# Routing logits of a mixture-of-experts stage: gate weights as the stationary operand, four column quadrants, and a transpose back

## The chip, the core and the metric

The kernel runs on one core of a Trainium2 chip. The metric is device time in microseconds of one execution; lower is better. A core has five engines with instruction queues of their own, each worked off in order: TensorE (PE; matmuls, with PEld for its weight loads), VectorE (DVE), ScalarE (ACT), GpSimd (POOL) and SyncE (SP, which here only issues DMAs). A matmul takes a stationary operand (the weights, loaded into the array first) and a moving operand (streamed through it column by column), and writes to PSUM.

## What is computed

All of it is f32, on 2 x 2048 tokens of 256 features, four residual steps in a row:

```python
x = x + attn_a(layernorm(x))      # causal attention, 16 heads of 16
x = x + ffn(layernorm(x))         # mixture of experts, first pass
x = x + attn_b(layernorm(x))      # softplus mixer, token by token
x = x + ffn(layernorm(x))         # the same mixture of experts, second pass
```

The mixture of experts, with E = 8 experts and the best two per token:

```python
logits = xt @ gate_w.T + gate_b                 # [tokens, 8]
scores = softmax(logits)
top_w, top_i = top_k(scores, 2)
gate_dense = sum(one_hot(top_i, 8) * top_w[..., None], axis=1)
outs = [(silu(xt @ w1[e].T + b1[e]) * (xt @ w3[e].T + b3[e])) @ w2[e].T + b2[e] for e in experts]
y = einsum('etd,te->td', outs, gate_dense)
z = silu(xt @ ws1.T + bs1) * (xt @ ws3.T + bs3) @ ws2.T + bs2      # shared expert, 512 wide
out = y + z
```

The change concerns the first line, the logits.

## The kernel before

**Stages.** The tokens are cut into eight chunks of 512 (`CH`), four per batch `b`; a chunk is four blocks of 128 tokens (`NB = 4`). X stays in SBUF throughout. Attention is the first stage. The second stage holds both passes of the mixture of experts (`f` is 0 or 1; the text calls them layer 0 and layer 1) and the mixer between them.

**Work of the second stage.** Generators emit its instructions:

- `route(f, c)` for one chunk: layer norm, transposes of the normalized tokens into feature-major form (`flipped`, tile `flip`, line 706, copied by ScalarE to `xT` at line 709), the gate's matmuls (line 736, tile `psl`), the add of the bias to the logits `lg` (line 741), and the ranks of the eight logits against each other (`ge`, lines 748 and 752) from which each token's two best experts come.
- `sort` and `weigh` for one batch: places in a list ordered by expert, and the softmax weights.
- `scatter` and `combine`: GpSimd's indirect DMAs that put the tokens in that order into DRAM (`xs`, line 868) and fetch the experts' results back (`yg`, line 895), which VectorE adds (line 908).
- `shared(f, c)`: the shared expert of one chunk (tiles `s`, line 986, and `sy`, line 1003).
- `routed(f, b)`: the experts, 39 blocks of 128 sorted tokens (loads at line 1035, transposes `tr` at 1045, copies `turned` at 1050, first matmuls `eu` at 1060, second matmuls `ed` at 1084).
- `mixer(c)`: the softplus step (matmuls `psz` at 936; the three ScalarE passes at 948, 949 and 959).

**Order.** The schedule is written out by the program itself, and each engine runs what it is given in that order. `shared` and `routed` are main work: one step of each in turn. `routing`, `moving` (scatter and combine) and `mixing` are side work. Each `yield (dve, act, pe, pool)` states what the next step is expected to cost on the four engines in us. A planner (`beside`) keeps a planned clock per engine, and after each main step it lets those side steps in whose engines are planned to be free soon and whose predecessor is planned to be done. For a step with a cost on PE the predecessor must be done within 0.2 us of PE's planned clock (`AHEAD`); for VectorE and ScalarE within 1.5 us. So the numbers in a yield decide where the instructions land in the queues, but waits at run time are made by semaphores alone. The routes of a batch run one after the other in one generator; those of layer 1 also wait for the mixer of their chunk, and experts of a batch start when its scatter is placed.

**The gate before.** The chunk's tokens are the stationary operand: for each of four token blocks and each of two halves of the features, 128 x 128 of `xT` are loaded as weights and the 8 columns of `gw_s` move through them. The result has tokens on partitions, 4 x 8 columns of one PSUM bank from `side_bank`, a pool of two banks that flips, gates, sorts and mixers share.

**The loads at the start of the stage.** SyncE issues the loads of `gw`, `gb`, `ws1`, `ws3`, the shared biases, `ws2` and the experts' weights in this order; GpSimd fills constant tiles at the same time.

Of the kernel before, what the change touches and what calls it, by code (L numbers as in the profile page):

```python
# [8 lines left out]
F32 = mybir.dt.float32  # L9
# [7 lines left out]
P = 128  # L17
# [7 lines left out]
NB = CH // P  # L25
NCH = N // CH
TC = B * NCH
E = 8
# [21 lines left out]
def hybrid_block(  # L50
# [23 lines left out]
    nc = tc.nc  # L74

    const = ctx.enter_context(tc.tile_pool(name="const", bufs=1))
    small = ctx.enter_context(tc.tile_pool(name="small", bufs=3))
# [13 lines left out]
    ident = const.tile([P, P], F32, tag="ident", name="ident")  # L91
# [45 lines left out]
    with tc.tile_pool(name="aw", bufs=1) as aw, ExitStack() as aw_ctx:  # L137
# [62 lines left out]
        def spectral(w, u, sp, cols, nm, bank):  # L200

            n = cols // P
            v = aw.tile([P, 2], F32, tag=f"v_{nm}", name=f"v_{nm}")
            for c in range(2):
                nc.vector.tensor_tensor_reduce(
                    wide(f"t_{nm}_{c}")[:, 0:cols], w[:, c, :], u, 1.0, 0.0, ALU.mult, ALU.add, v[:, c:c + 1]
                )
            ps = bank(f"psr_{nm}")
            for m in range(n):
                for c in range(2):  # L210
                    nc.tensor.matmul(
                        ps[:, m:m + 1], w[:, c, m * P:(m + 1) * P], v[:, c:c + 1],
                        start=c == 0, stop=c == 1,
                    )
            r = aw.tile([P, n], F32, tag=f"r_{nm}", name=f"r_{nm}")
            nc.vector.tensor_copy(r, ps[:, 0:n])

            s = aw.tile([P, 2], F32, tag=f"s_{nm}", name=f"s_{nm}")
            nc.vector.tensor_mul(v, v, v)
            nc.vector.tensor_mul(r, r, r)  # L220
            nc.vector.reduce_sum(s[:, 0:1], v, axis=AX.X)
            nc.vector.reduce_sum(s[:, 1:2], r, axis=AX.X)
            ps = bank(f"pss_{nm}")
            nc.tensor.matmul(ps[:, 0:2], ones, s, start=True, stop=True)

            f = aw.tile([P, 1], F32, tag=f"f_{nm}", name=f"f_{nm}")
            ru = aw.tile([P, 1], F32, tag=f"ru_{nm}", name=f"ru_{nm}")
            nc.vector.reciprocal(f, ps[:, 0:1])
            nc.vector.tensor_mul(f, f, ps[:, 1:2])
            nc.gpsimd.tensor_tensor(ru, f, nhalf[:, 0:1], ALU.pow)  # L230
            nc.vector.tensor_mul(f, f, ru)
            nc.vector.reciprocal(f, f)
            nc.vector.tensor_mul(f, f, sp)
            return f

        with ExitStack() as ac:
# [266 lines left out]
            nm, na = 0, 0  # L503
# [7 lines left out]
            f = factors["k"] = spectral(*loaded, 3 * D, "qkv", bank)  # L511
# [9 lines left out]
            while na < len(units) or due or behind:  # L521
# [12 lines left out]
                if run_m:  # L534
# [13 lines left out]
                    kc, i = mx.pick(cols)  # L548
# [19 lines left out]
                if run_m:  # L568
# [10 lines left out]
                    if not mx.left:  # L579
                        shift(*w, mx.part, nmax[nm % 2])  # L580
                        ready[nm] = tick[0] + LAG
                        mx, nm = None, nm + 1
# [3 lines left out]
    fw = ctx.enter_context(tc.tile_pool(name="fw", bufs=1))  # L586
# [8 lines left out]
    def weight(src, shape, nm, eng):  # L595
        t = fw.tile(shape, F32, tag=nm, name=nm)
        eng.dma_start(t, src)
        return t

    def row(src, n, nm, eng):  # L600
        t = fw.tile([P, n], F32, tag=nm, name=nm)
        eng.dma_start(t, src.partition_broadcast(P))
        return t

    gw_s = weight(gw, [P, 2, E], "gw", nc.sync)
    gb_s = row(gb, E, "gb", nc.sync)
    ws1_s = weight(ws1, [P, 2, SH], "ws1", nc.sync)
    ws3_s = weight(ws3, [P, 2, SH], "ws3", nc.sync)
# [48 lines left out]
    def side_bank(nm):  # L657
        return ps_x.tile([P, CH], F32, tag="px", name=nm)
# [8 lines left out]
    def feature_major(nm):  # L667
        while live[0] >= XTS:
            yield None
        live[0] += 1  # L670
        return cw.tile([P, 2, CH], F32, tag="xT", name=f"xT_{nm}", bufs=XTS)

    def token_major(nm):
        while held[0] >= XNS:
            yield None
        held[0] += 1
        return cw.tile([P, NB, D], F32, tag="xn", name=f"xn_{nm}", bufs=XNS)

    def normed(xc, xn, nm):
        st = small.tile([P, NB, 6], F32, tag="lnst", name=f"lnst_{nm}")  # L680
        mv = small.tile([P, NB, 2], F32, tag="lnmv", name=f"lnmv_{nm}")
        ve = small.tile([P, NB], F32, tag="lnve", name=f"lnve_{nm}")
        rs = small.tile([P, NB], F32, tag="lnrs", name=f"lnrs_{nm}")
        for h in range(2):
            yield (0.9, 0, 0, 0)
            for i in range(2 * h, 2 * h + 2):
                nc.vector.bn_stats(st[:, i, :], xc[:, i, :])
                nc.vector.bn_aggr(mv[:, i, :], st[:, i, :])
            if h == 1:
                nc.vector.tensor_scalar_add(ve, mv[:, :, 1], EPS)  # L690
        yield (0, 0, 0, 1.2)
        nc.gpsimd.tensor_tensor(rs, ve, nhalf, ALU.pow)
        for h in range(2):
            yield (0.75, 0, 0, 0)
            for i in range(2 * h, 2 * h + 2):
                nc.vector.tensor_scalar(
                    xn[:, i, :], xc[:, i, :], mv[:, i, 0:1], rs[:, i:i + 1],
                    ALU.subtract, ALU.mult,
                )

    def flipped(xn, xT, nm):
        yield (0, 1.2, 0.9, 0)
        for d in range(2):
            ps = side_bank(f"flip_{nm}_{d}")
            for i in range(NB):
                nc.tensor.transpose(
                    ps[:, i * P:(i + 1) * P], xn[:, i, d * P:(d + 1) * P], ident
                )
            nc.scalar.copy(xT[:, d, :], ps)

    def route(f, c):

        b, q = divmod(c, NCH)
        nm = f"{f}_{c}"
        while f == 1 and c not in mixed:
            yield None
        if q == 0:
            scores[f, b] = rw.tile([P, BLK, E], F32, tag="lg", name=f"lg_{f}_{b}", bufs=1)
            picks[f, b] = rw.tile([P, TOPK, BLK, E], F32, tag="pick", name=f"pick_{f}_{b}", bufs=1)
            sel[f, b] = rw.tile([P, E, BLK], BF16, tag="sel", name=f"sel_{f}_{b}", bufs=1)  # L720
        blk = slice(q * NB, (q + 1) * NB)
        xn = yield from token_major(f"f{nm}")
        yield from normed(X[c], xn, f"f{nm}")
        xhat[f, c] = xn
        yield (0, 0, 0, 2.4)
        nc.gpsimd.tensor_tensor(
            X[c], X[c], bs2_s.unsqueeze(1).to_broadcast([P, NB, D]), ALU.add
        )
        xT = yield from feature_major(f"f{nm}")
        yield from flipped(xn, xT, f"f{nm}")  # L730
        xhatT[f, c] = xT
        yield (0.2, 0, 1.8, 0)
        ps = side_bank(f"psl_{nm}")
        for i in range(NB):
            for d in range(2):
                nc.tensor.matmul(  # L736
                    ps[:, i * E:(i + 1) * E], xT[:, d, i * P:(i + 1) * P], gw_s[:, d, :],
                    start=d == 0, stop=d == 1,
                )
        lg = scores[f, b][:, blk, :]  # L740
        nc.vector.tensor_tensor(
            lg, ps[:, :NB * E].rearrange("p (n e) -> p n e", e=E),
            gb_s.unsqueeze(1).to_broadcast([P, NB, E]), ALU.add,
        )
        yield (1.6, 0, 0, 0)

        ge = small.tile([P, NB, E, E], F32, tag="ge", name=f"ge_{nm}", bufs=2)
        nc.vector.tensor_tensor(
            ge, lg.unsqueeze(2).to_broadcast([P, NB, E, E]),
            lg.unsqueeze(3).to_broadcast([P, NB, E, E]), ALU.is_ge,  # L750
        )
        nc.vector.tensor_tensor(
            ge, ge, before.unsqueeze(1).to_broadcast([P, NB, E, E]), ALU.mult
        )
        up = small.tile([P, NB, E], F32, tag="rup", name=f"rup_{nm}", bufs=2)
        dn = small.tile([P, NB, E], F32, tag="rdn", name=f"rdn_{nm}", bufs=2)
        nc.vector.reduce_sum(up, ge, axis=AX.X)
        nc.vector.reduce_sum(dn, ge.rearrange("p n e j -> p n j e"), axis=AX.X)
        yield (0.6, 0, 0, 0)
        nc.vector.tensor_tensor(up, up, dn, ALU.subtract)  # L760
        pk = picks[f, b]
        for k in range(TOPK):
            nc.vector.tensor_tensor(
                pk[:, k, blk, :], up, level[:, k, :].unsqueeze(1).to_broadcast([P, NB, E]),
                ALU.is_equal,
            )
        nc.vector.tensor_tensor(
            sel[f, b][:, :, blk].rearrange("p e n -> p n e"), pk[:, 0, blk, :], pk[:, 1, blk, :],
            ALU.add,
        )  # L770
# [353 lines left out]
    def routing():  # L1124
        for f, b in rows:
            for c in chunks(b):
                yield from route(f, c)
            yield from sort(f, b)
            yield from weigh(f, b)
# [59 lines left out]
    while sides or todo or shares or mains:  # L1189
# [15 lines left out]
        name = sorted(mains)[turn_of % len(mains)]  # L1205
# [79 lines left out]
```

## Time and profile before

| | us |
|---|---|
| median of 3 runs | 2157.02 (2152.82 to 2159.84) |
| the profiled execution: time | 2150.73 |
| its span, first to last instruction | 2148.8 |
| attention, to the last matmul of its projection | about 1181 |
| second stage, first PE instruction | 1187.1 |
| the 16 gates, first to last | 1191.7 to 1912.8 |
| scatter of the last batch | 1923.5 to 1963 |
| experts of the last batch end on PE | about 2095 |
| last instructions | 2149 |

A page of the profile has busy times of each engine, the span in 40 slices with the busy share of each in tenths, the chain of waits that ended last, and groups of like instructions by source line. A group's line reads: source line, engine, operation, output tile <- input tiles, shapes, count | busy us, mean ns of one | idle time of the engine just before them, and what ended it. Starts and lengths in a timeline or in the chain are us from the span's start. An f32 matmul leaves two records (and two weight loads) on PE, an f32 transpose one. Ends of matmuls are modelled, since they are pipelined, so distances between starts tell more than lengths. TensorE's granted clock was 0.98 of full over the span and 0.98 to 1.00 in the stretches of the second stage between 1187 and 2100 us, except 0.91 from 1960 to 1980.

The gate's own rows, from the groups by line:

| line | engine, operation | count | median ns |
|---|---|---|---|
| 736 | PEld LDWEIGHTS psl, 128x128 | 256 | 192 |
| 736 | PE MATMUL psl, 128x8 moving | 256 | 256 |
| 741 | DVE TENSOR_TENSOR lg, 128x32 | 16 | 191 |
| 748 | DVE TENSOR_TENSOR ge, 128x256 | 16 | 425 |

### The profile page before, as it was taken

The numbers are of one execution on the slowest core, as the hardware profiler recorded it, in microseconds if no ns is written. First come the engines' busy times: TensorE is split into PE (matmuls) and PEld (weight loads), VectorE is DVE, ScalarE is ACT, GpSimd is POOL, SyncE is SP. The second block draws the span as 40 slices with busy tenths as digits, with TensorE's granted clock in tenths as the row PEclk, the third lists the DMA queues.
The fourth block names the chain that finished last, engine by engine and source line by source line (L and its number), as shares of the span: only waits on it lengthen the run. The fifth ranks groups of instructions, "written<-read, shape, count | busy, mean of one in ns | idle before, by whom it ended". The sixth has DMA issues, their size and how long they took to land.

```text
span 2148.8 us, 36170 instructions
## 1 busy us (share of the span) xinstructions
PE 2026.7 (94%) x11840; PEld 1091.1 (51%) x11840; DVE 1384.1 (64%) x3424; ACT 1074.9 (50%) x1566; POOL 872.9 (41%) x1157
## 2 busy tenths in 40 slices
PE   6899999999999999999999999999999999999993
PEld 3444444444444444444444566665656566655662
DVE  2567777777676777777871455545777368763643
ACT  0437577757776757767876122233353234341330
POOL 3325344524444434434445263603432753336305
PEclk9899999999999999999999999999999999999997
DMA  2111110000000000000000511323210332103524
GB/s 93 48 49 36 45 51 16 7 6 6 3 7 6 6 4 4 6 4 4 2 2 1 217 61 64 136 76 118 84 40 25 114 112 85 35 30 131 173 73 122
DMA packets 87587, 113.04 MB, mean 53 GB/s; under 512 B 16368, under 2 KB 75120, under 8 KB 87280
## 3 DMA queue, kind: packets, MB, share of 16 engines
q1 hardware_dynamic: 74000, 75.60, 11.1%
q0 software_dynamic: 12288, 33.57, 4.7%
q8 instruction: 101, 1.65, 0.3%
q10 hardware_dynamic: 1120, 1.57, 0.2%
q14 instruction: 78, 0.64, 0.1%
HBM read 54.59 MB, written 51.64 MB: 49 GB/s over the span
## 4 chain that ended last, share of the span: by engine, by line
PE 80%; DVE 7%; POOL 4%; issue 4%; ACT 3%; DMA 1%; DVEq 0%; SPq 0%; POOLq 0%; ACTq 0%
PE st L378 15%; PE o L397 13%; PE psm L333 13%; PE eu L1060 10%; PE s L986 7%; PE ed L1084 5%; PE sy L1003 4%; PE psk L267 3%; PE tr L1045 2%; PE psz L936 1%; PE psj L446 1%; POOL xs L868 1%; PE psv L293 1%; DVE junk L342 1%; PE psl L736 1%
## 5 line engine op out<-in xcount | busy, mean ns | idle before, releaser
L382 ACT ACTIVATE pt<-st 128x1024 f32<-128x1024 f32 (+3 forms) x640 | 555.8, 895 | 189.8 <-PE psm L333 129.9
L333 PE MATMUL psm<-kT,qT 32*128 32x512 f32 (+3 forms) x2560 | 627.1, 570 | 15.0 <-DMA kT<-sk 8.9
L378 PE MATMUL st<-qT,kT 32*128 32x512 f32 (+3 forms) x2560 | 610.7, 557 | 1.3 <-ACT pt L382 1.3
L347 DVE TENSOR_REDUCE part<-psm 128x1 f32<-128x512 f32 x768 | 477.4, 682 | 121.5 <-PE psm L333 117.3
L408 POOL TENSOR_TENSOR oa<-oa,op 128x512 f32<-128x512 f32 (+3 forms) x288 | 312.8, 1086 | 454.4 <-ACT op L406 454.4
L378 PEld LDWEIGHTS st<-qT,kT 32*128 32x128 f32 x2560 | 266.1, 186 | 225.9 <-ACT pt L382 137.8
L342 DVE CUSTOM_DVE_ANT_0 junk<-psm,maskq 128x384 bf16<-128x384 f32 (+3 forms) x512 | 250.8, 490 | 112.0 <-PE psm L333 47.7
L333 PEld LDWEIGHTS psm<-kT,qT 32*128 32x128 f32 x2560 | 276.1, 186 | 86.2 <-issue 27.1
L397 PE MATMUL o<-pt,v 128*32 128x512 f32 (+3 forms) x2560 | 304.2, 545 | 12.1 <-DVE part L347 5.6
L1060 PE MATMUL eu<-we,turned 128*128 x560 | 263.7, 593 | 0.0
L1067 ACT ACTIVATE es<-ea 128x256 f32<-128x256 f32 x156 | 65.0, 417 | 357.9 <-DVE ea L1065 357.8
L986 PE MATMUL s<-xT_f,ws 128*128 128x512 f32 x512 | 231.4, 595 | 0.0
L895 POOL DMA_INDIRECT yg<-ys,slot x128 | 128.1, 1001 | 234.3 <-DVE x L908 74.0
L385 POOL TENSOR_SCALAR_AFFINE_SELECT pt<-pt 128x256 f32<-128x256 f32 x256 | 102.3, 407 | 211.6 <-ACT pt L382 207.7
L406 ACT COPY op<-o 128x512 f32<-128x512 f32 (+3 forms) x288 | 148.3, 515 | 64.1 <-PE o L397 48.8
L1065 DVE TENSOR_TENSOR ea<-eu,be 128x512 f32<-128x512 f32 x156 | 107.4, 688 | 111.0 <-PE eu L1060 110.4
L1084 PE MATMUL ed<-we,turned 128*128 x624 | 162.6, 383 | 14.5 <-ACT turned L1050 14.5
L397 PEld LDWEIGHTS o<-pt,v 128*32 128x32 f32 x2560 | 52.5, 108 | 218.0 <-DVE part L347 123.4
L1084 PEld LDWEIGHTS ed<-we,turned 128*128 128x128 f32 x624 | 116.2, 190 | 87.9 <-issue 48.3
L868 POOL DMA_INDIRECT xs<-xn_f,slot x128 | 124.7, 974 | 85.1 <-DVE slot L822 57.9
L986 PEld LDWEIGHTS s<-xT_f,ws 128*128 128x128 f32 x512 | 94.8, 191 | 102.0 <-issue 95.4
L1060 PEld LDWEIGHTS eu<-we,turned 128*128 128x128 f32 x560 | 97.6, 191 | 75.0 <-issue 73.1
(266 smaller groups left out, 2111.0 us busy)
## 6 DMA issues: line engine op xcount, KB each, us to landing
xs<-xs SPq DMA_DIRECT2D x156, 128.0 KB
ys<-ey SPq DMA_DIRECT2D x156, 128.0 KB
xs<-zeros SPq DMA_DIRECT2D x78, 128.0 KB
we<-in_we_dram SPq DMA_DIRECT2D x8, 768.0 KB
x<-in_x_dram SPq DMA_DIRECT2D x8, 512.0 KB
kT<-sk SPq DMA_DIRECT2D x128, 32.0 KB
out_dram<-x SPq DMA_DIRECT2D x8, 512.0 KB
be<-in_be_dram SPq DMA_DIRECT2D x1, 3072.0 KB
```

The source lines that it names most:

```text
L333: nc.tensor.matmul(ps[:, :n], self.q[r, i * P:(i + 1) * P], kT[b, g, kc][r, :n], start=True, stop=True,)
L342: nc.vector.tensor_tensor_reduce(junk[:, :n], ps[:, :n], maskq[:, CH - n:], 1.0, LOW, ALU.add, ALU.max, m,)
L347: nc.vector.reduce_max(m, ps[:, :n], axis=AX.X)
L378: nc.tensor.matmul(st[:, i, off:], k[r, ks], q[r, off:], start=True, stop=True)
L382: nc.scalar.activation(pt[:, :, off:], st[:, :, off:], AF.Exp)
L397: nc.tensor.matmul(o[32 * j:32 * j + 32, off:], V[kb // NB][:, kb % NB, 4 * g + j, :], pts[j // 2][:, j % 2, off:], start=True, stop=True,)
L406: nc.scalar.copy(t[:, off:], o[:, off:])
L408: nc.gpsimd.tensor_tensor(a[:, off:], a[:, off:], t[:, off:], ALU.add)
L868: ins = nc.gpsimd.indirect_dma_start(out=XS[b], out_offset=bass.IndirectOffsetOnAxis(ap=slots[f, b][:, k, n:n + 1], axis=0), in_=xhat[f, b ...
L986: nc.tensor.matmul(ps, w[:, d, cs], xT[:, d, :], start=d == 0, stop=d == 1)
L1060: nc.tensor.matmul(ps, t[:, 1, d * P:(d + 1) * P], we_s[:, bass.ds(v + d * CH, CH)], start=d == 0, stop=d == 1,)
L1084: nc.tensor.matmul(ps[:, 0:D], t[:, 0, d * P:(d + 1) * P], we_s[:, bass.ds(v + 2 * CH + d * D, D)], start=d == 0, stop=d == 1,)
```

## The change

- `gw_s` becomes 32 columns wide; GpSimd sets it to zero and the load fills columns 0 to 7 of each half of the features.
- The gate's operands change places. `gw_s` (128 features x 32 columns) is the stationary operand, and 128 tokens of `xT` move. Token block i writes partitions 32 i to 32 i + 31 of the bank (a column quadrant of the array), and the loop over the halves of the features is now outside that over the blocks.
- ScalarE copies the 128 x 128 result to a new SBUF tile `lt` (one buffer), TensorE transposes it into a second side bank, and VectorE adds the bias from there, reading 8 of every 32 columns.
- The planner's step (0.2, 0, 1.8, 0) becomes two: (0, 0.3, 0.6, 0) ahead of the matmuls and the copy, and (0.2, 0, 0.2, 0) ahead of the transpose and the add.
- `ge` has one buffer where it had two.

```diff
-    gw_s = weight(gw, [P, 2, E], "gw", nc.sync)
+
+    gw_s = fw.tile([P, 2, 32], F32, tag="gw", name="gw")
+    nc.gpsimd.memset(gw_s, 0.0)
+    nc.sync.dma_start(gw_s[:, :, 0:E], gw)
...
-        yield (0.2, 0, 1.8, 0)
+        yield (0, 0.3, 0.6, 0)
+
         ps = side_bank(f"psl_{nm}")
-        for i in range(NB):
-            for d in range(2):
+        for d in range(2):
+            for i in range(NB):
                 nc.tensor.matmul(
-                    ps[:, i * E:(i + 1) * E], xT[:, d, i * P:(i + 1) * P], gw_s[:, d, :],
+                    ps[32 * i:32 * i + 32, 0:P], gw_s[:, d, :], xT[:, d, i * P:(i + 1) * P],
                     start=d == 0, stop=d == 1,
                 )
+        lt = small.tile([P, P], F32, tag="lt", name=f"lt_{nm}", bufs=1)
+        nc.scalar.copy(lt, ps[:, 0:P])
+        yield (0.2, 0, 0.2, 0)
+        ps = side_bank(f"pst_{nm}")
+        nc.tensor.transpose(ps[:, 0:P], lt, ident)
         lg = scores[f, b][:, blk, :]
         nc.vector.tensor_tensor(
-            lg, ps[:, :NB * E].rearrange("p (n e) -> p n e", e=E),
+            lg, ps[:, 0:P].rearrange("p (n e) -> p n e", e=32)[:, :, 0:E],
             gb_s.unsqueeze(1).to_broadcast([P, NB, E]), ALU.add,
         )
         yield (1.6, 0, 0, 0)
 
-        ge = small.tile([P, NB, E, E], F32, tag="ge", name=f"ge_{nm}", bufs=2)
+        ge = small.tile([P, NB, E, E], F32, tag="ge", name=f"ge_{nm}", bufs=1)
```

## The prediction of the time

> **What bounds the kernel now.** I read the page's busy shares, its 40 slices and its chain of waits first.
>
> ```profile
> PE 2026.7 (94%) x11840; PEld 1091.1 (51%) x11840; DVE 1384.1 (64%) x3424; ACT 1074.9 (50%) x1566; POOL 872.9 (41%) x1157
> ...
> PE   6899999999999999999999999999999999999993
> ...
> PE 80%; DVE 7%; POOL 4%; issue 4%; ACT 3%; DMA 1%; DVEq 0%; SPq 0%; POOLq 0%; ACTq 0%
> ```
>
> TensorE is busy in every slice but the ends and carries 80% of the chain. The change lies in the second stage, from 1187 us on; attention before it keeps its instructions. So I went to the stage: the chain around one gate (the eight logits matmuls of a 512-token chunk, tile psl).
>
> ```profile
> 1206.58 1.73 PE sy L1003 x8
> 1208.31 1.69 PE psl L736 x16
> 1209.99 2.04 PE sy L1003 x9
> ```
>
> The columns are start, length, engine, tile, line, records (an f32 matmul leaves two records, a transpose one). The gate sits between other matmuls with no hole on either side: what it gives up, the next matmul takes. Summing the holes of over 0.25 us between PE records from 1187 to 2110 us gives 35.6 us, 6.5 of them before the stage's first transposes; nearly everything else is queued PE work. The windows agree: 1187 to 1316 us holds 128.9 us of PE in 129, 1500 to 1700 holds 194.6 in 200, 1700 to 1900 holds 187.8. Sixteen gates at 1.70 us are 27.2 us of PE.
>
> **Why a gate costs 1.70 us.** Each of its 16 records streams 8 columns only, but loads 128 columns of tokens as weights. The records start 0.112 us apart, the pace of the loads (LDWEIGHTS median 0.192 us, two in flight); 16 x 0.112 = 1.79 us, of which 1.703 is measured from the first matmul to the next group's first, since the first load is hidden.
>
> **What replaces it.** Weights of 32 columns, four quadrants side by side, 128 token columns moving: 16 records again, as four bunches of four (two halves of f32, two halves of the 256 features). The nearest row is the attention's value product on a diagonal block, the same shape (128*32, 128 moving) with 8 records, in the timeline of PE alone:
>
> ```profile
> 239.71 0.43 PE L397 MATMUL o<-pt,v 128*32 128x128 f32 x8
> 240.07 0.70 PE L378 MATMUL st<-qT,kT 32*128 32x512 f32 x2
> ```
>
> From its first start to the next group's first start: 0.36 us (0.356 in the records, in 25 places). Its four quadrants start 0.007 us apart, and the second bunch 0.135 us after the first. Two bunches more make 0.356 + 2 x 0.134 = 0.624.
>
> **Rule against row.** The Trainium skill, "TensorEngine Tiling (Array Packing)", section Key Properties, speaks against the change: going from one tiling mode to another drains the array, and here every gate stands between full-array matmuls, so it pays two switches. It gives no price; the trace does. A last 512-column score matmul to the first value matmul takes 0.517 us against 0.427 of stream (four records of a shared matmul take 1.72): 0.09 going in. A last 384-column value matmul to the transposes behind it: 0.416 against 0.320, 0.10 going out, already inside the 0.356. After the way out, the first weight load isn't hidden: 0.166 to the next start in place of 0.109, 0.06 more. So a gate is 0.09 + 0.624 + 0.06 = 0.77 us. Read at its hardest, with each bunch waiting for the modelled end of the one before (0.297 us), it would be 4 x 0.297 + 0.15 = 1.34 us and the saving 4 us in all; the rows don't show that between bunches, so I take 0.77.
>
> **The transpose back** is one more 128x128 record on the full array, in a row with others 0.109 us: 0.11. PE per chunk: 0.77 + 0.11 = 0.88 against 1.70, 0.82 saved, **13.1 us for 16 chunks**, if all of it is on the path.
>
> **The copy to lt.** ScalarE gets 16 copies of 128x128 out of PSUM. Its row:
>
> ```profile
> L406 ACT COPY op<-o 128x128 f32<-128x128 f32 x32 | 8.7, 271 | 4.3 <-PE o L397 4.3
> ```
>
> 16 x 0.27 = 4.3 us on an engine that is half idle: no cost by itself. But the transpose waits for it at the head of PE's queue, with the experts' and shared matmuls behind. The planner's new step keeps the transpose back until at least one main step has gone by: 1.3 or 1.72 us of PE (two expert groups or four shared records) over a copy of 0.27 plus semaphores. The cover fails where ScalarE is caught in a mixer's softplus (1.06 + 1.28 table load + 1.06 = 3.4 us): up to 2.1 us per chunk, at most 8 chunks (those of layer 1) = 16.8 us; the other end is 0. The like case exists already, the gate behind the copy of its transposed tokens:
>
> ```profile
> PE ed L1084 <- ACT turned L1050: 14.5, 16, 1.7
> ...
> PE tr_-4_17531 L1045 <- DMA xs<-xs: 2.7, 1, 2.7
> PE tr_-4_15657 L1045 <- DMA xs<-xs: 2.0, 1, 2.0
> PE psl L736 <- ACT xT_f L709: 1.3, 2, 0.8
> ```
>
> (total us, times, longest). 1.3 us over 16 gates, and I take **1.3 us** for the new wait too.
>
> **Later scores.** Logits were ready 1.89 us after the gate's start (1.70 plus 0.19); now 0.77 + one main step 1.72 + 0.11 + about 0.25 of semaphore and start = 2.85: 1.0 us later, 2.7 with two steps between. VectorE works in order, so what stands behind the add waits only if it was planned early; it was moved with it. The chunk's lateness matters where sort and scatter are waited for. The chain at the last batch:
>
> ```profile
> 1961.52 0.96 POOL xs L868
> ...
> 1962.78 2.37 DMA xs<-xn_f,slot
> ...
> 1965.61 3.00 DMA xs<-xs
> ...
> 1968.65 0.53 PE tr_-3_17538 L1045 x2
> 1969.18 3.33 PE sy L1003 x8
> ```
>
> GpSimd writes tokens one scatter after the other, and PE stands at the first transposes of the experts (2.7 + 0.9 us; 2.0 at the batch before, 1714 us). There a chunk that is 1.0 us late is 1.0 us lost: **2.0 us** for the two batches of layer 1 (bounds 0 and 5.4). But see what follows at 1969: shared matmuls are still left when the experts start, so a PE that is ahead doesn't run dry, it has fewer of them left. In layer 0 the scatter is covered by eight shared chunks of 20.7 us each, so its lateness costs nothing.
>
> **Small edits.** The zeroing of gw stands first on GpSimd (the first memset there takes 0.15 us), and SyncE's load of gw now waits for it, with gb, ws1, ws3 and the experts' weights queued behind; GpSimd's own memsets push the first normalization power (1185.48), which the stage's first transposes wait for. Both shift by 0.15 to 0.3: **0.2 us**, lower end 0, since PE waits there already. The load now lands in 32-byte pieces; it is first used 10 us later. One ge buffer in place of two: writer and readers are all on VectorE in order, no waits are shown at those lines: 0. Two side banks per chunk where there was one, out of two: the next transposes wait until lt or the logits are read; within the 1.3 above. The planner's own numbers fall from 1.8 to 0.8 us per chunk, near the real change, but they move every later instruction's place; that is worth some us either way and goes to the range.
>
> **Sum.** -13.1 + 1.3 + 2.0 + 0.2 = -9.6 us. The profiled execution has a span of 2148.8 and a time of 2150.73 us, so 1.9 us lie around the span; it would become 2141.1. It lies 6.3 us below the median of 2157.02; the same ratio (0.9955) on the median gives **2147.4 us**. About 0.3%, 6.5 us, is what a measurement of this kernel can tell from no change.
>
> **Rivals.**
> *Only layer 0 counts (2154.0 us, no change).* In layer 1 the mixers' chain and the scatter set when experts start (gates at 1811, 1848, 1886, 1911 us, each right after its mixer), so time saved on PE is waited away at 1714 and 1965 us. Left are 8 x 0.82 = 6.5 less the 3.5 us of costs: -3.0. For it: PE already waits there. Against: shared matmuls are left after both waits.
> *The score chain decides (2165.7 us, slower).* The extra ScalarE hop and PE visit put two main steps into each route, 2.7 us, and the four routes of a batch run in one generator, so both scatters of layer 1 slip by 4 x 2.7 = 10.8 us, with PE idle: -13.1 + 0.2 + 21.6 = +8.7. It decides from 1.6 us per route ((13.1 - 0.2) / 8). For it: 40 us of scatter follow the last gate. Against: layer 1's routes start 23 to 48 us apart behind mixers, so only the last one's lateness should reach the scatter.
> *The quadrants don't run at once, or the drain is dear:* 1.34 us a gate, the saving 4 us, costs 3.5: 2156.5, no change. The value product speaks clearly against it.
>
> **Chances.** Forecast 0.56; no change 0.23 (0.18 layer 0 only, 0.05 the drain); slower 0.21, of which a bad new order of instructions without that mechanism is part. Range 2140 to 2164: low is the full 13.1 without costs (2143.9) less 3.5 us of scatter between runs, high reaches just short of the slower rival's centre. The forecast alone: 2142 to 2151.
>
> **What would show it.** Gates of 16 records 128*32 with 128 moving, taking about 0.8 us on PE from first start to the next group's, with PE's busy time some 12 us less; transposes' waits for lt of 1 to 2 us in all; the first experts' transposes of the last batch still waiting 3 to 5 us, shared matmuls still behind them, and the whole stage shorter by the difference. Wrong if a gate takes over 1.3 us, if the wait for lt is over 0.8 us per chunk, or if the wait for the scatter grows by 10 us.

## The result, and the profile after

The changed kernel takes **2160.86 us** (median of 13 runs, 2159.07 to 2166.38) against 2155.23 us of the kernel before on the same chip (13 runs, 2149.11 to 2159.84). The ratio of the means is **1.0036, 95% interval 1.0024 to 1.0049**, or 7.8 us. The executions of either kernel fall into two groups some 5 us apart, so that the medians lie only 5.6 us apart. It is slower, by nearly as much as the forecast (0.9955) had it faster. The profiled execution took 2159.73 us, with a span of 2157.7 us, 9.0 us above the one of before.

TensorE did become less busy. The busy shares, the row of TensorE in the 40 slices, and the chain by engine, from the page of after:

```profile
PE 2011.7 (93%) x11856; PEld 1067.2 (49%) x11856; DVE 1382.3 (64%) x3424; ACT 1079.1 (50%) x1582; POOL 874.7 (41%) x1158
...
PE   5899999999999999999998999999999999999990
...
PE 77%; DVE 7%; POOL 6%; issue 4%; ACT 3%; DMA 2%; DVEq 0%; SPq 0%; ACTq 0%; POOLq 0%
```

15.0 us of TensorE are gone from the sum. But the last digit went from 3 to 0: work that TensorE did at the very end, in the last 54 us, is done earlier now. And 3% of the chain has left TensorE for GpSimd and DMA.

The gate itself takes what the forecast expected. TensorE's timeline of after around one gate (start, length, engine, line, operation, output<-inputs, shape, records):

```profile
1206.03 1.89 PE L1012 MATMUL sy<-ws,hsh 128*128 128x256 f32 x8
1207.85 0.64 PE L740 MATMUL psl<-xT_f,gw 128*32 128x128 f32 x16
1208.42 1.99 PE L1012 MATMUL sy<-ws,hsh 128*128 128x256 f32 x8
1210.26 0.27 PE L748 MATMUL pst<-ident,lt 128*128 128x128 f32 x1
1210.36 3.17 PE L995 MATMUL s<-xT_f,ws 128*128 128x512 f32 x7
```

From the gate's first start to the next group's first start 0.57 us pass. The first quadrant matmul starts 0.095 us later than it would in an unbroken stream (523 ns in place of 427 behind a 512-column record), and behind the gate the next group's second record starts 0.106 us later. Together this is 0.776 us, and the transpose takes 0.11 us. The four bunches of quadrant matmuls start 0.134, 0.109 and 0.109 us apart.

The old gate had a surcharge of the same kind, which the forecast left out: in before the first record behind a gate takes 0.513 us in place of 0.427. So the old gate cost 1.70 + 0.09 = 1.79 us, and the saving is 16 x (1.79 - 0.89) = 14.4 us rather than 13.1.

So I compared when things happen in the second stage. All times are us from the first TensorE instruction of the stage (1187.1 before, 1183.8 after); a sort is timed by its first matmul, a scatter by its last DMA instruction; "first transposes" are those of each expert batch, (layer, batch), which wait for that batch's scatter.

| | before | after |
|---|---|---|
| gates of layer 0, first batch | 4.6, 21.0, 37.5, 54.1 | 5.1, 24.0, 43.0, 61.9 |
| last gate of layer 1 | 724.1 | 738.7 |
| first sort, last sort | 61.0, 731.1 | 69.6, 745.7 |
| last instruction of the first scatter, of the last | 110.1, 775.7 | 121.1, 790.4 |
| first transposes (0,0), (0,1), (1,0), (1,1) | 117.3, 273.4, 529.7, 780.2 | 125.6, 273.7, 537.4, 796.7 |
| experts' end on TensorE | 908.5 | 924.7 |
| end of the stage | 961.7 | 973.9 |

A gate follows the one ahead of it after 16.5 us before, and after 18.9 us now: each route takes 2.4 us longer, where the forecast had 1.0. The last scatter ends 14.7 us later. In layer 1 the delay begins anew: the first gate there stands at 375.6 us against 375.4, the fourth is 6.9 us late, the fifth 11.9 and the last 14.6. And still TensorE isn't idle much longer. From the waits of TensorE in after, 1187 to 2110 us (total us, times, longest):

```profile
PE ed L1093 <- ACT turned L1059: 17.0, 17, 3.1
PE sy L1012 <- DVE hsh L1000: 5.4, 4, 2.4
PE tr_-4_15730 L1054 <- DMA xs<-xs: 4.2, 1, 4.2
PE tr_-4_13789 L1054 <- DMA xs<-xs: 3.0, 1, 3.0
PE tr_-4_12569 L1054 <- DMA xs<-xs: 2.9, 1, 2.9
PE pst L748 <- issue: 1.7, 1, 1.7
...
PE pst L748 <- ACT lt L745: 0.2, 1, 0.2
```

The new transposes cost 1.9 us of waiting in all, near the 1.3 of the forecast; only 0.2 of it is shown to be for `lt`, and for the other 1.7 the profile names no cause. The longest wait for a scatter is 4.2 us. What fills the rest shows in TensorE's timeline. First before, where the last experts end:

```profile
2094.49 1.13 PE L1084 MATMUL ed<-we,turned 128*128 x4 [0.52 <-ACT turned L1050]
2095.46 13.90 PE L986 MATMUL s<-xT_f,ws 128*128 128x512 f32 x32
2109.19 7.07 PE L1003 MATMUL sy<-ws,hsh 128*128 128x256 f32 x32
```

and then after, where they begin, and where they end (the last line is the last one of TensorE):

```profile
1980.51 0.38 PE L1054 MATMUL tr_-4_17647<-ident,xs 128*128 128x128 f32 x2
...
1980.95 1.89 PE L1012 MATMUL sy<-ws,hsh 128*128 128x256 f32 x8
1982.68 1.88 PE L1069 MATMUL eu<-we,turned_-4_17650 128*128 x4
1984.40 1.89 PE L1012 MATMUL sy<-ws,hsh 128*128 128x256 f32 x8
```

```profile
2106.51 0.38 PE L1054 MATMUL tr<-ident,es 128*128 128x128 f32 x2
2107.41 1.13 PE L1093 MATMUL ed<-we,turned 128*128 x4 [0.52 <-ACT turned L1059]
```

Before, one whole shared chunk (13.9 + 7.1 us; the last one, number 7 of layer 1) comes after the experts, while GpSimd fetches the experts' results back: it is hidden there. After, that chunk is done ahead of and beside the first experts, and the end of TensorE's work is the end of the experts. So the sum for the end of the experts is +20.7 (the chunk now ahead) - 14.4 (the gates) + 5.5 (holes of over 0.25 us: 34.6 in place of 29.1) + 0.9 (smaller holes) + 3.8 (TensorE's granted clock) = +16.5 us, against +16.2 in the table. The clock's term is an estimate: from the start of the stage to the end of the experts the granted clock is half for 21.3 us in after and for 13.8 us in before, and half of the difference is lost. (A second profile of before, e13, has 17.8 us, so part of that term may be the execution's.) The tail behind the experts is 4 us shorter, so the stage is 12.2 us longer than in before, and 9.3 us longer than in e13. The run up to the stage is 3.3 us shorter, which leaves the 9.0; that part isn't the change's doing (last section).

**Where the order comes from.** The planner's numbers in its own clock, worked out from the program and not from a trace, tell both shifts. Before, a route in layer 0 takes eight main steps from gate to gate. In the changed kernel the new step waits for one more, and each gate moves TensorE's planned clock by 0.8 us in place of 1.8. VectorE's steps of the layer norm are due 1.85 us ahead of that clock and so no longer fit the window of 1.5 us: they wait for one more main step too, and a route takes ten. The first gates stand 18.9 us apart in the trace, which is ten steps of the 1.72 us of the plan plus the route's own work on TensorE. For the shared chunk this rule decides (lines 1192 to 1194 of before):

```python
wait = "experts" in mains or (todo and todo[0] in placed)
if fit and (live[0] >= XTS or not wait):
    mains["share"] = shared(*fit[0])
```

Before, the last experts are placed at 780.9 us of the planned clock while shared chunk 6 runs until 796.5, so chunk 7 must wait for the experts. After, chunk 6 ends at 782.0 and the experts are placed only at 792.3: for these 10 us nothing stands against chunk 7, and it starts.

### The profile page after: what moved, and what is told of

Read it like the earlier page. It is cut to its first block, busy times and chain, and to the rows that moved or that the text cites. A ratio compares the mean times of both kernels' runs of the same rounds, so it can differ in the third digit from the quotient of the medians.

```text
span 2157.7 us, 36240 instructions
## 1 busy us (share of the span) xinstructions
PE 2011.7 (93%) x11856; PEld 1067.2 (49%) x11856; DVE 1382.3 (64%) x3424; ACT 1079.1 (50%) x1582; POOL 874.7 (41%) x1158
## 4 chain that ended last, share of the span: by engine, by line
PE 77%; DVE 7%; POOL 6%; issue 4%; ACT 3%; DMA 2%; DVEq 0%; SPq 0%; ACTq 0%; POOLq 0%
PE st L378 15%; PE o L397 13%; PE psm L333 12%; PE eu L1069 10%; PE s L995 6%; PE ed L1093 5%; PE sy L1012 3%; PE psk L267 3%; POOL xs L877 3%; PE tr L1054 2%; PE psz L945 1%; PE psj L446 1%; DVE junk L342 1%; PE psv L293 1%; DMA yg<-ys,slot 1%
```

## The experiments

Two theories were to be told apart, and the gate as a third. **Order, by place:** the time is lost since shared chunk 7 has left its cover. **Order, by lateness:** it is lost since each route, and with it each scatter, comes later. **The gate:** the new gate itself costs more than it saves.

All runs but e13, e14 and e15 were on chips on which the kernel before takes 2233 to 2240 us, with engines that stand still during the scatters (last section). So only ratios to runs of the kernel before on the same chip are compared.

### Gate and order apart

e1 has the new gate in the order of before (one planner step with the old numbers), e2 the old gate in the order of after (the two new steps around the old matmuls):

```diff
 # e1, against after
-        yield (0, 0.3, 0.6, 0)
+        yield (0.2, 0, 1.8, 0)
...
-        yield (0.2, 0, 0.2, 0)
 # e2 and e11, against before
-        yield (0.2, 0, 1.8, 0)
+        yield (0, 0.3, 0.6, 0)
...
+        yield (0.2, 0, 0.2, 0)
```

> New gate in one planner step with the old numbers (0.2, 0, 1.8, 0): matmuls, copy, transpose and add directly behind one another, so that every other instruction keeps the place it has before the change. Order theory (the planner's two new steps moved the work, the quadrants themselves are cheap): the gate with its open wait for the copy takes about 1.2 + 0.11 us of PE from its first start, 0.1 going in and 0.03 going out, against 1.70, so 16 x 0.27 = 4 us less: 2151 us (2146 to 2155), and the starts of the four expert batches stand where they stand before, within 4 us. Hardware theory (the quadrants, the extra copy or the second bank cost the time): 2160 us or more, as after the change.

> Old gate (tokens as weights, no copy, no transpose) in the planner's two new steps with the new numbers: matmuls in the first, add of the bias in the second; all other instructions stand where they stand after the change. Order theory: it loses what the change loses and saves nothing on PE, so up to 13 us above the changed kernel where PE is the bound: 2168 us (2163 to 2176), the experts of the last batch about 15 us later than before, and the last shared chunk ahead of their end. Hardware theory: 2155 us, as before the change.

> The changed kernel itself, so that it can be set against the runs beside it on the same chip. A ratio to before of 1.0036 (1.002 to 1.006), as measured first.

> Old gate in the order of the changed kernel (two planner steps), once more. Order theory on a chip like the first: all of the loss and none of the saving, 1.0036 + 13/2155 = 1.0096 at most, 1.007 to 1.010. Hardware theory: 1.000.

| ratio to before (95%) | order of before | order of after |
|---|---|---|
| old gate | 1 | e2 1.0129 (1.0111 to 1.0147), e11 1.0108 (1.0093 to 1.0124) |
| new gate | e1 1.0054 (1.0039 to 1.0070) | e5 1.0078 (1.0062 to 1.0094) |

The order of after costs 1.2% with the old gate. That is more than expected (1.0096 at most). Within that order the new gate gains 0.4% (mean of e2 and e11 less e5), 9 us of the 14.4. Within the order of before it loses, where a gain of 4 us was expected. The waits of TensorE in e1 tell why (total us, times, longest):

```profile
PE pst L746 <- ACT lt L744: 23.3, 16, 4.5
```

With no step between gate and transpose, TensorE stands at all 16 transposes until ScalarE has copied `lt`: about 0.4 us where ScalarE is free, and up to 4.5 where it is in a mixer's softplus. 23.3 - 14.4 = +8.9 us on 2233 is 1.0040, at the lower end of the measured interval. So the second planner step is needed, and it is what moves the order.

### The last shared chunk

The hold keeps shared chunk 7 of layer 1 back until the experts are done; e4 does the opposite to the kernel before.

```diff
 # hold: e3, e12 and e18, against after
             fit = [s for s in shares if s in xhatT]
+            if fit and fit[0] == (1, TC - 1) and (todo or "experts" in mains):
+                fit = []
 # e4, against before
-            if fit and (live[0] >= XTS or not wait):
+            if fit and (live[0] >= XTS or not wait or fit[0] == (1, TC - 1)):
```

> The changed kernel, but the last shared chunk (layer 1, chunk 7) is held until the last experts are done, as it happens to be before the change. Order theory: in the changed kernel this chunk fills the wait for the last scatter for about 10 us and takes another 10 us from the experts; held, the experts end 8 to 12 us earlier and its 20.7 us of PE lie beside the final gather, whose tail becomes 4 us longer: 2155 us (2151 to 2158). Scatter theory (the last scatter alone sets the end, the shared chunk is free filling): no change, 2161 us.

> The kernel before, but the last shared chunk may start while the last experts run, and so ends before them; the gate is the old one. Order theory: its 20.7 us of PE go into the path, 4 us of tail come back: 2171 us (2166 to 2176). Scatter theory: within 3 us of before, 2155 us.

> The changed kernel with the last shared chunk held until the last experts are done, once more. Order theory on a chip like the first: 1.000 (0.998 to 1.002), as on the second (0.9999). Scatter theory: 1.0036.

> The changed kernel with the last shared chunk held, once more beside e16 and e17. Lateness theory (later scatters are most of the loss on a chip like the first): old gate in this order with the hold is at 1.0085, less the new gate's 13 us of 2155, 1.0025 (1.001 to 1.005). Place theory: 0.998 or less.

With the hold the changed kernel went from 1.0078 (e5) to 0.9999 (0.9983 to 1.0014), 0.9974 (0.9962 to 0.9986) and 1.0001 (0.9988 to 1.0013): mean 0.9991. Letting the chunk go in the kernel before costs as much: 1.0074 (1.0058 to 1.0090). On these chips the chunk's place makes up the changed kernel's loss, seen from both sides. But even with it put right the changed kernel only draws level: the gates' 14.4 us (0.6%) don't show.

### The planner's numbers

If the missed window of 1.5 us makes the routes late, a wider one should bring the eight steps back. e8 tries the other number: the old gate in one step, planned at 0.8 us, with the hold.

```diff
 # e6 and e9 against after, e7 and e10 against before
-    AHEAD = (1.5, 1.5, 0.2, 2.7)
+    AHEAD = (1.8, 1.5, 0.2, 2.7)
 # e8, against before, with the hold besides
-        yield (0.2, 0, 1.8, 0)
+        yield (0.2, 0, 0.8, 0)
```

> The changed kernel with one number of the planner changed: a side step for VectorE may be emitted when its predecessor is planned to be done within 1.8 us, not 1.5. Order theory: the extra step of the change puts the later VectorE steps of a route just past 1.5 us, so that a route takes ten main steps where it took eight; at 1.8 it is eight again, the gates of layer 0 stand about 14.7 us apart, the last experts start ahead of where they start before the change, the last shared chunk comes after them again, and the 13 us saved on PE show: ratio to before 0.995 (0.993 to 0.9975). Scatter or hardware theory (what follows the gate, or the gate itself, costs the time): 1.000 or more.

> The kernel before with the same number, 1.8: the control. Order theory: its routes already take eight main steps, so no change, ratio 1.000 (0.998 to 1.002). If it gains as much as the changed kernel does from this number, the gain has nothing to do with the change.

> Old gate in one step as before, but with the planned cost on PE lowered from 1.8 to 0.8 us as in the change, and the last shared chunk held until the last experts are done: the new numbers without the second step. Order theory: the number alone does little, ratio 1.000 (0.998 to 1.003), gates of layer 0 within 1 us of where they stand before. Rival (the planner's too low number is what delays the routes): 1.004 or more.

> The changed kernel with the planner's 1.5 us for VectorE raised to 1.8, once more, in the hope of a chip on which the engines don't stand still for 20 us during each scatter, as they did beside e5 to e8 (before: 2235 us there, 2155 us in the first measurement). Order theory on a chip like the first: ratio 0.995 (0.993 to 0.998). On one like the second: 1.004 (1.002 to 1.006) again. Scatter or hardware theory: 1.002 or more on both.

> The kernel before with 1.8, the control, once more. Order theory on a chip like the first: 1.000 (0.998 to 1.002); on one like the second 1.0036 again, since there the gain or loss hangs on what the engines are doing when they stop.

The wider window gave 1.0042 (1.0029 to 1.0055) and 1.0023 (1.0012 to 1.0034) with the change, and 1.0036 (1.0022 to 1.0049) and 1.0028 (1.0017 to 1.0038) without it: with this window the change makes no difference that can be told, and neither kernel is better than before. The 0.995 hoped for in e6 didn't come, nor the no change in e7, though in both shared chunk 7 is behind the experts. Why the kernel before loses by the window isn't known. What e6 does show is the window's part in the routes: its first four gates stand at 5.1, 24.0, 41.3 and 58.5 us, so from the second on a route takes 17.3 us in place of 18.9, nine main steps. The window costs one of the two steps, and the new planner step the other. e8 gave 0.9986 (0.9975 to 0.9996), with gates at 5.1, 21.5, 37.9 and 54.5 us: the smaller number alone leaves the routes as early as they were, so it takes the extra step to make them late.

### On a chip like that of the first comparison

Here the kernel before takes 2153.63 us (whether it is the same chip isn't on record). e13 is the kernel before once more. e14 is the order of after with the old gate (e2's edit) and the hold: with the chunk in its place, only lateness is left, though more of it than in the changed kernel, since the old gates are longer (the last sort is 10 us later than in after). e15 is the changed kernel with the hold and wider windows, so that the routes come early again:

```diff
 # e15, against after, with the hold besides
-    LEAD = (1.7, 1.3, 0.0, 2.7)
-    AHEAD = (1.5, 1.5, 0.2, 2.7)
+    LEAD = (2.0, 1.3, 0.0, 2.7)
+    AHEAD = (2.1, 1.5, 0.2, 2.7)
```

> The kernel before itself, beside its own runs: ratio 1.000 (0.998 to 1.002), which says how far two sets of runs of one kernel lie apart here, and its trace shows whether it too stands still during the scatters on this chip.

> Old gate in the order of the changed kernel, with the last shared chunk held until the last experts are done. Place theory (the loss is that this chunk moved ahead of the experts' end): the order's loss of 1.0118 falls by the 0.009 that holding brought the changed kernel, to 1.003 (1.001 to 1.005), and what is left above the changed kernel with hold (0.9987) is the saving of the new gate, 9 to 13 us. Lateness theory (the routes' two more main steps and the later scatters are the loss): 1.007 or more.

> The changed kernel with the hold and with both thresholds of the planner for VectorE raised (predecessor due within 2.1 us, engine free within 2.0 us), which puts the start of the last experts in the planner's clock 24 us ahead of the changed kernel's. Lateness theory: 0.989 to 0.993. Place theory: as with the hold alone, 0.997 to 1.000.

| | ratio (95%) | last sort | first transposes (1,1) | experts' end | stage end |
|---|---|---|---|---|---|
| e13 | 0.9997 (0.9986 to 1.0009) | 732.5 | 781.6 | 911.5 | 964.6 |
| e14 | 1.0085 (1.0071 to 1.0100) | 755.7 | 804.9 | 928.2 | 981.6 |
| e15 | 0.9961 (0.9946 to 0.9976) | 723.5 | 772.4 | 899.0 | 952.2 |

e14 speaks against the place alone: chunk 7 is back behind the experts, and 18 us are lost all the same. TensorE's waits in the second stage of e14 say where much of it lies:

```profile
PE ed L1085 <- ACT turned L1051: 14.8, 15, 2.5
PE tr_-4_17542 L1046 <- DMA xs<-xs: 11.8, 1, 11.8
PE tr_-4_15681 L1046 <- DMA xs<-xs: 3.9, 1, 3.9
```

11.8 us of idle TensorE at the first transposes of the last experts, against 2.8 in e13: their scatter comes later, and no shared chunk is left to fill the time. TensorE is slow there as well: from 1978 to 1998 us, the wait and what follows it, its granted clock was 0.66. So the chunk's move in the changed kernel goes with the lateness: for the late scatter TensorE either waits, or does the chunk that would have been hidden behind the experts.

An estimate for the changed kernel with the hold on this chip can be put together from the traces: the last scatter instruction at 790.4 us (after), 4.7 us from there to the first transposes, 123.3 us of experts and a tail of 53.4 us (all three from e14) make a stage of 972 us. That is 2 us less than without the hold and still 7 to 10 us above before and e13, so on such a chip most of the loss would be lateness.

e15 turns both round. Its scatter comes 8 to 9 us earlier than in before and e13, the chunk stays behind the experts, and from TensorE's waits in its second stage nothing large is left at the transposes:

```profile
PE pst L748 <- ACT lt L745: 4.9, 4, 2.0
PE tr_-4_17596 L1054 <- DMA xs<-xs: 1.7, 1, 1.7
...
PE tr_-4_15697 L1054 <- DMA xs<-xs: 1.2, 1, 1.2
```

The experts end 9.5 to 12.5 us earlier than in before and e13. Its ratio of 0.9961 is the best of all runs, and where the forecast (0.9955) had put the change, but it falls short of the 0.989 to 0.993 that the lateness theory had expected. Its first gates stand 17.2 us apart, so a route takes nine main steps and not eight. That the gate is what it owes this to isn't shown by e15 alone: the windows and the hold with the old gate were not run on this chip, nor was the changed kernel with the hold alone, so how the 0.4% divides between the gate and the order stays open.

### The windows on the other chips

e16 and e17 are before and after with `AHEAD` at 1.8 and `LEAD` at 2.0, without the hold.

> The kernel before (old gate, one step) with the planner's thresholds for VectorE at 1.8 and 2.0 us. The last experts are then placed before the two last shared chunks start, so both lie beside the final gather. Place theory: the experts end 20.7 us earlier in the planner's clock (897.9 against 918.6), the tail grows by up to 5 us: ratio 0.992 (0.990 to 0.997). If the scatter can't be met that early and PE waits for it: 0.997 or more.

> The changed kernel (new gate, two steps) with the same thresholds, 1.8 and 2.0 us; the main work stands in the same sequence as in e16. The new gate's own worth where the order isn't spoiled: the planner's clock is another 11.2 us ahead (886.7 against 897.9), so 0.005 below e16 (0.003 to 0.007), 0.987 in all. If nothing of the 13 us of PE reaches the end: the same as e16.

1.0047 (1.0034 to 1.0061) and 1.0045 (1.0031 to 1.0060): the two gates can't be told apart, and both are slower than before, where 0.992 and 0.987 were expected. So on these chips an earlier order did not help, and neither theory holds there as a whole (e18, too, lay between the two values expected). The gate's gain shows on these chips only at the fixed late order (e5 against e2 and e11). That would fit engines which stand still at each scatter, since TensorE's time saved ahead of it can be waited away there; this was not shown.

## Why the prediction was wrong

- **The gate, 1.70 to 0.77, and 0.11 for the transpose:** right for the new gate, 0.776 and 0.11. The quadrants run at once, and the two switches cost what the attention's rows had shown. The old gate was put too low: 16 x 0.112 = 1.79 was its cost, since the load that is hidden on the way in shows behind the gate (0.09 us). So the saving was 14.4 us, not 13.1; TensorE's busy sum fell by 15.0.
- **The wait for `lt`, 1.3 us:** right at 1.9. Its cover, the main step in between, is real: e1, without it, paid 23.3 us, with up to 4.5 us at one transpose, more than the 2.1 that the forecast had as its bound.
- **Later scores, 2.0 us:** this is the step that failed. It priced the new planner step by what it delays in its own chunk, 1.0 us at run time, and counted only the last chunk of each batch of layer 1. The planner doesn't delay by a time but by whole main steps, and what comes behind in the same generator misses its window as well: ten steps per route in place of eight, 2.4 us for each route of layer 0's first batch. The first sort is 8.6 us later, and where 2.0 us were counted for layer 1 the last sort is 14.6 us later and the last scatter 14.7.
- **"In layer 0 ... its lateness costs nothing":** wrong. Eight gates had saved about 7 us when layer 1 began, and yet its first gate stands where it stood (375.6 us against 375.4). Around the first experts of layer 0 TensorE waits 4.6 us where before has no such wait (the 1.7 and the 2.9 in the list above), and its granted clock from 1290 to 1340 us was 0.97 in place of 1.00. Most of the saving of layer 0 went there. Its lateness didn't reach layer 1, which made its own.
- **"A PE that is ahead doesn't run dry, it has fewer of them left":** true, and that is where the price lay. What it has fewer of is shared work behind the last experts, which was free there. I had seen that chunk (TensorE's last 21 us) and not asked what rule keeps it last.
- **The planner's numbers, "worth some us either way", to the range:** these were the largest term, and the same failed step seen from the plan: +20.7 us for one chunk, against 14.4 saved. Held back, the chunk would have left a wait in its place. Both could have been worked out ahead of the run, in the planner's own clock.
- **Rivals.** "The score chain decides" had the right mechanism, routes of 2.7 us more each (2.4 measured), and the right sign; it expected TensorE idle, and the time went into the moved chunk instead: 2165.7 predicted, a ratio of 1.0040 to the median it was worked from, against 1.0036. That the number agrees so closely is luck in part. I held against it that layer 1's routes stand apart behind mixers; but these slipped as well. "The drain is dear" is out by the gate's own records. "Only layer 0 counts" is out by the sign.

So the saving was real, and a worse order outweighed it: it cost some 24 to 27 us, if the stage's 9.3 to 12.2 us are put on top of the 14.4 saved; e2 and e11 have 1.2% for it, 26 us. Shown are the gate's saving, the late routes, the moved chunk and the loss from each of the two order effects (e4 and e5 against the held runs, e14). Shown too is what makes the routes late: the two steps with the old gate do it (e2), the smaller number alone doesn't (e8), and the wider window alone takes back one of the two main steps (e6). Not shown is how the loss divides between place and lateness on a chip like the first: there the only run with earlier routes, e15, changed two windows and the hold together.

## What to carry to other kernels

Where a program lays out its own order, a new or cheaper step has two prices, that of its instructions and that of the order it brings about; the second is found by following the planner's clock through the thresholds, before the run. Ask of every piece of work that is hidden now which rule puts it there and by how much margin: here 16 us of planned time decided whether 21 us of TensorE lay behind the experts or ahead of them. And a wait that is covered by a step in between (0.2 us for `lt`) must be priced with and without the cover, since the step that covers it is the one that delays the rest.

## What the runs showed of the hardware

**Chips of two kinds.** The same program took 2152 to 2157 us on some chips and 2233 to 2240 on others. The difference lies in the scatters. The kernel before on a chip of the first kind (e13) and the changed one on another (e5), 28 us around the second scatter (its instructions start from 1355 to 1395 us in e13, from 1364 to 1406 in e5); the columns are the stretch, its length, the busy times of TensorE, its loads, VectorE, ScalarE and GpSimd, then granted clock, DMA share and GB/s:

```profile
1372.00:1400.00 28.00, 28.00 (x115) 17.93 (x114) 13.70 (x29) 8.98 (x18) 20.15 (x38) 1.00 0.53 180
```

```profile
1372.00:1400.00 28.00, 7.44 (x18) 3.81 (x16) 2.46 (x5) 1.42 (x3) 21.05 (x41) 0.64 0.30 105
```

TensorE is busy for 28 of 28 us on one and for 7.4 on the other. The DMA queues in the same stretch (packets, MB, share of the 16 engines), in before and then in e5:

```profile
q1 hardware_dynamic: 2763, 2.52, 28.9%
q0 software_dynamic: 872, 2.36, 21.4%
```

```profile
q0 software_dynamic: 987, 2.67, 27.1%
q1 hardware_dynamic: 288, 0.26, 3.0%
```

GpSimd's queue moves about as much on both, but in e5 the other queue, that of SyncE's loads and stores, gets a tenth of its packets through. At the four scatters TensorE's holes of over 1 us come to 8, 28, 25 and 23 us in e5, 84 us together, which is about what lies between the two kinds. The slow queue isn't the whole cause, though. At the fourth scatter of e5 no experts are at work, and yet ScalarE stands:

```profile
2030.76 3.78 PE L995 MATMUL s<-xT_f,ws 128*128 128x512 f32 x4 [5.85 <-issue]
2041.08 0.69 ACT L997 ACTIVATE hsh<-s,bs 128x512 f32<-128x512 f32 x1 [18.21 <-remote]
```

The activation reads `s`, whose last matmul ends by 2034.6 us, and begins at 2041.1, after 18.2 us of idle ScalarE; the profile names no instruction of this core that it waits for. What stops the engines on such chips, no run here shows.

**The way to the stage.** The second stage starts at 1183.3 to 1184.9 us in nine of the 20 traces and at 1187.1 to 1189.9 in the other eleven, though attention's instructions are the same in all. It isn't the order that decides: e8, with the routes of before, starts at 1183.3, and e11 and e12, with the order of after, at 1189.9 and 1188.9. What goes with it is TensorE's granted clock over the first 60 us: 0.93 to 1.00 in the nine, 0.86 to 0.91 in the eleven. What sets that isn't shown. In the first comparison the profile of after is of the early kind and that of before of the late one, which makes the change look 3 us better in the profiles than it is.
